# Cross attentions with 16 heads of 16: turning the exponents, or taking the scores a second time with keys on partitions

## The chip, the cores and the metric

The kernel runs on one core of a Trainium2 chip. The metric is the device time in microseconds (us) of one launch. Times of groups of instructions come from one profiled execution; a kernel's time is the median of its timed runs. The engines are TensorE (PE, its weight loads PEld), VectorE (DVE), ScalarE (ACT), GpSimd (POOL), and SyncE (SP), which starts DMAs.

## What is computed

The reference is a decoder of four layers on x of shape (8, 112, 256), each with a self attention, a cross attention and a feed-forward part, all in float32 but for a quantised last part. The change concerns the cross attentions of layers 1 and 3. Both attend from the 112 tokens of each batch to the 375 rows of a context of width 128, with 16 heads of 16:

```
B, LQ, D_MODEL = q.shape
...
qh = (q @ Wq + bq).reshape(B, LQ, HEADS, D_K).transpose(0, 2, 1, 3)
kh = (k @ Wk + bk).reshape(B, LKV, HEADS, D_K).transpose(0, 2, 1, 3)
vh = (v @ Wv + bv).reshape(B, LKV, HEADS, D_K).transpose(0, 2, 1, 3)
```

Then softmax(qh kh^T / 4) vh for each head, the heads joined, times Wo (plus bo), and added to x. Here q is the layer-normalised x, and k and v are both the context. Layer 3 has the same form without biases.

## The kernel before, in words

A class holds x on chip and runs the twelve sublayers in turn. `cross` (line 1098) serves three of them: layers 1 and 3 with heads of 16 (`dense`), and a part of layer 2 with heads of 32 that the change leaves as it is.

Work goes in 32 steps (b, c): b is one of 8 batches, c one of four chunks of four heads. A chunk's queries lie on 128 partitions, four strips of 32 rows. In the dense case two heads share the 32 rows of a key strip, so a batch has two key tiles of 128 rows instead of four; a query strip holds one head's 16 rows and zeros for the other's (`_halves`, line 79), and the order of heads that this needs (`_SLOTS`, line 71) is also applied to the value and output weights.

Before the loop come the keys and values of batch 0, `ln_T` (line 465: normalise half of the tokens, transpose them on TensorE, copy them), four query products for the first half of the tokens, and `ln_T` for the second half. This part is ordered by the framework's own scheduler. In the loop (lines 1250 to 1283) the order on TensorE, VectorE and ScalarE is the written one. One step does:

- `turn` (1183): for each of the chunk's four heads three transposes of the exponents (line 1187) into one of two PSUM banks "tr", then one copy to SBUF, on VectorE (1195) for even heads and on ScalarE (1193) for odd ones;
- `key` (1129) for the next batch in steps 0 and 2, `summed` (1215) in step 1, `divide` (1227) in step 3 for the batch before;
- `score` (1162) for the next step: four matmuls of 32 rows, queries stationary and keys moving, so that tokens lie on partitions and the 375 keys along the row; one PSUM bank each;
- `exponent` (1169): for each head the negated row maximum on VectorE (1174) and exp(score - maximum) on ScalarE (1178);
- `value` (1139) for the next batch in steps 0 to 2; two `query` products for the second half in step 3 of batches 0 and 1; `result` (1238) for the batch before in step 3: the output product and `finish`, here `add_to_x` (489);
- `attend` (1198): twelve matmuls, three chunks of 125 keys for each head, values (32 columns a head, column 16 holding ones, so that sums of exponents come along) stationary, exponents moving. After step 3 the outcome goes to SBUF on ScalarE (1213).

`summed` gathers the sums of exponents by four small matmuls, takes reciprocals (1222) and spreads them on POOL (1224); `divide` transposes them (1230) and multiplies (1236). Key, value, query, sums and result share a single PSUM bank "mm". All plain matmuls pass through the helper `mm`, and so carry its line, L410 in the profile.

Of the kernel before, what the change touches and what calls it, by code (L numbers as in the profile page):

```python
# [66 lines left out]

_SLOTS = [8 * (n // 2) + 2 * j + n % 2 for n in range(4) for j in range(4)]


def _slots(w):

    return w.reshape(-1, 16, 16)[:, _SLOTS].reshape(w.shape)


def _halves(w):

    out = np.zeros((w.shape[0], 4, 4, 2, 16), w.dtype)
    a = w.reshape(-1, 16, 16)[:, _SLOTS].reshape(-1, 4, 4, 16)
    for n in range(4):
        out[:, n, :, n % 2] = a[:, n]
    return out.reshape(-1, 512)
# [29 lines left out]
def _weights(inp):  # L115
    def g(layer):
# [49 lines left out]
            ("l1x_wq", _fm(_halves(xa("Wq")))),  # L166
            ("l1x_wk", xa("Wk")),
            ("l1x_wv", _slots(xa("Wv"))),
            ("l1x_bv", _row(_slots(xa("bv")[None])[0])),
        ],  # L170
        [
            ("l1x_wo", _fm(_spread(_slots(xa("Wo").T)).T)),
# [7 lines left out]
    for j in range(2):  # L180
# [4 lines left out]
        ("l1x_bq", _col(_halves(xa("bq")[None])[0])),  # L185
        ("l1x_bk", _col(xa("bk"))),
# [42 lines left out]
    v2 = [(f"l2f_{n}_s", _col(f(f"{n}_s"))) for n in ("w1", "w2", "h1", "h2")]  # L229
    for pf in ("a1", "a2"):  # L230
        for n in ("lnx_g", "lnx_b", "lny_g", "lny_b", "ln3_g", "ln3_b", "li2_b"):
# [12 lines left out]
            ("l3x_wq", _fm(_halves(xa("Wq").T))),  # L244
            ("l3x_wk", wkv[:, :D]),
            ("l3x_wv", _slots(wkv[:, D:])),
            ("l2f_w3_s", _row(inp["L2_ffn_w3_s"])),
        ],
        [("l3x_wo", _fm(_spread(_slots(xa("Wo"))).T))],
# [106 lines left out]
class _Kernel:  # L356
# [741 lines left out]
    def cross(self, name, cT, qsrc, wq, wk, wv, wo, hd, scale, finish, ctx, bq=None, bk=None, bv=None):  # L1098


# [18 lines left out]

        values = [self.t(acts, [P, NCH, 16, 32], f"xv{i}") for i in range(2)]  # L1120
        dense = hd == 16
        nk = 2 if dense else 4
        if dense:
            for v in values:
                nc.gpsimd.memset(v, 0.0)
                nc.gpsimd.memset(v[:CH, :, :, hd : hd + 1], 1.0)
        keys = {}

        def key(b, c):
            if c == 0:  # L1130
                keys[b] = self.t(work, [P, nk, CTX], "xkT")
            pm = self.t(ps1, [P, 512], "mm")[:, :CTX]
            self.mm(pm, [(wk[:, c * P : (c + 1) * P], cT[:, b * CTX : (b + 1) * CTX])])
            if bk is None:
                nc.scalar.copy(keys[b][:, c, :], pm)
            else:
                nc.scalar.activation(keys[b][:, c, :], pm, AF.Identity, bias=self.v(bk, c))

        def value(b, i):
            pm = self.t(ps1, [P, 512], "mm")[:CH, : 16 * hd]  # L1140
# [1094 lines left out]
```

## Time and profile before

| | us |
|---|---|
| three timed runs | 2417.11, 2418.55, 2422.47 (median 2418.55) |
| profiled execution, its own time | 2413.31 |
| its span in the trace | 2411.5 |
| layer 1's cross attention, first scores to first output product of the tail | 828.7 to 1003.1 |
| layer 3's cross attention, first scores to the tail's output product | 2121.2 to 2295.6 |
| one inner batch of either | 19.48 |

A row of the timeline gives the start and length in us, the engine, the line, the operation, the tile written and those read, their shapes (stationary, then moving), and the count; in brackets idle time before it and who ended it. A row of busy times gives a stretch, its length, then PE, PEld, DVE, ACT and POOL with counts, the granted TensorE clock, the DMA share and GB/s. "L1187" is a line of the kernel.

### The profile page before, as it was taken

What the parts mean: (1) busy time and instruction counts of PE and PEld (TensorE: products, weight loads), DVE (VectorE), ACT (ScalarE), POOL (GpSimd) and SP (SyncE); (2) the same over time, 40 slices, a digit from 0 to 9 for tenths busy, and PEclk for the clock granted to TensorE, in tenths of its full rate; (3) what the DMA queues carried; (4) which work ended last, traced back from release to release, by engine and by line L of the source; (5) the groups of instructions that cost most, each with busy time, mean ns of one, the idle gap of its engine ahead of it and who ended that gap; (6) DMA issues with size and microseconds to landing.
All of it is one profiled execution on the core that took longest, in us unless ns stands there. A gap on an engine that the chain in (4) does not pass through costs nothing.

```text
span 2411.5 us, 43235 instructions
## 1 busy us (share of the span) xinstructions
PE 2138.1 (89%) x17032; PEld 1268.5 (53%) x17032; DVE 1430.9 (59%) x3994; ACT 773.9 (32%) x2157; POOL 217.1 (9%) x415
## 2 busy tenths in 40 slices
PE   6999999989898899899898859899999999899944
PEld 3444444445556566646555536466655556556622
DVE  4655566565545567553888557767750133667787
ACT  2333334453211256430111211366321110246522
POOL 0111111000011100000222331100000000200000
PEclk9999999899999999999999989999999999899966
DMA  4000000000100000101001001000111100000000
GB/s 186 2 2 2 2 20 35 30 18 18 53 1 15 19 2 2 36 9 35 35 18 35 19 27 53 18 1 2 71 35 53 51 0 1 1 1 2 2 0 16
DMA packets 10730, 55.94 MB, mean 23 GB/s; under 512 B 1833, under 2 KB 3625, under 8 KB 5792
## 3 DMA queue, kind: packets, MB, share of 16 engines
q1 hardware_dynamic: 8304, 44.57, 5.2%
q0 software_dynamic: 2080, 7.07, 0.9%
q8 instruction: 135, 2.21, 0.4%
q10 hardware_dynamic: 144, 1.54, 0.2%
q14 instruction: 67, 0.55, 0.1%
HBM read 52.23 MB, written 0.92 MB: 22 GB/s over the span
## 4 chain that ended last, share of the span: by engine, by line
PE 67%; DVE 21%; issue 5%; ACT 4%; DMA 2%; POOL 1%; DVEq 0%; ACTq 0%; POOLq 0%
PE mm L410 31%; PE gu L410 6%; PE g L649 6%; PE tr L1187 6%; PE sc L410 4%; PE av L1203 3%; PE tr L410 2%; DVE rot L1496 1%; ACT sg L660 1%; PE av L786 1%; PE av L410 1%; ACT th L671 1%; DVE hT L675 1%; PE g L627 1%; PE s L410 1%
## 5 line engine op out<-in xcount | busy, mean ns | idle before, releaser
L649 PE MATMUL g<-w,hT 128*32 128x256 f32 x3552 | 237.3, 384 | 26.0 <-DVE hT L675 25.8
L1174 DVE TENSOR_REDUCE xnm<-sc 112x1 f32<-112x375 f32 x384 | 184.6, 541 | 28.5 <-PE sc L410 28.0
L1187 PEld LDWEIGHTS tr<-cst,xe 112*125 112x125 f32 x1152 | 151.5, 188 | 94.7 <-issue 37.9
L1187 PE MATMUL tr<-cst,xe 112*125 112x112 f32 x1152 | 192.9, 289 | 7.2 <-DVE xeT L1195 4.3
L410 PE MATMUL mm<-xnT,w 128*128 128x448 f32 x432 | 182.3, 559 | 18.8 <-DVE qT L1499 5.3
L410 PE MATMUL mm<-hT,w 128*128 128x448 f32 x512 | 193.0, 539 | 0.0
L649 PEld LDWEIGHTS g<-w,hT 128*32 128x32 f32 x3552 | 95.4, 109 | 168.1 <-DVE hT L675 124.9
L410 PEld LDWEIGHTS mm<-hT,w 128*128 128x128 f32 x512 | 97.1, 190 | 94.4 <-issue 94.4
L627 PE MATMUL g<-xw,cst 128*32 128x256 f32 x1792 | 138.0, 379 | 0.0
L1195 DVE COPY xeT<-tr 125x336 f32<-125x336 f32 x192 | 97.3, 507 | 67.6 <-PE tr L1187 60.7
L1193 ACT COPY xeT<-tr 125x336 f32<-125x336 f32 x192 | 85.4, 445 | 159.9 <-PE tr L1187 159.9
L410 PEld LDWEIGHTS mm<-xnT,w 128*128 128x128 f32 x432 | 77.8, 192 | 104.0 <-issue 54.0
L1178 ACT ACTIVATE xe<-sc,xnm 112x375 f32<-112x375 f32 x256 | 126.4, 582 | 11.2 <-DVE xnm L1174 11.2
L410 PE MATMUL mm<-w,hT 128*112 128x256 f32 x576 | 129.0, 383 | 0.0
L410 PE MATMUL gu<-xnT,w 128*128 128x448 f32 x320 | 126.1, 549 | 1.6 <-DVE hT L1341 1.2
L410 PE MATMUL mm<-w,oT 128*112 128x256 f32 x416 | 105.6, 404 | 22.2 <-DVE oT L1676 13.7
L410 PEld LDWEIGHTS mm<-w,hT 128*112 128x112 f32 x576 | 102.0, 179 | 25.3 <-issue 3.5
L660 ACT ACTIVATE sg<-g 128x192 f32<-128x192 f32 x224 | 74.1, 331 | 104.8 <-PE g L649 92.7
L671 ACT ACTIVATE th<-cell 128x64 f32<-128x64 f32 x224 | 57.4, 256 | 147.4 <-DVE cell L669 147.1
L410 PEld LDWEIGHTS mm<-w,oT 128*112 128x112 f32 x416 | 74.1, 186 | 52.1 <-DVE oT L1676 15.0
L2089 DVE COPY wq<-tr 128x256 bf16<-128x256 bf16 (+1 forms) x12 | 4.6, 420 | 162.9 <-PE tr L2088 162.9
L673 DVE TENSOR_TENSOR h<-sg,th 128x64 f32<-128x64 f32 x224 | 50.6, 226 | 85.5 <-ACT th L671 85.5
(402 smaller groups left out, 3631.4 us busy)
## 6 DMA issues: line engine op xcount, KB each, us to landing
w<-in_w SPq DMA_DIRECT2D x33, 1024.0 KB, 4.9
raw<-in_wq POOLq DMA_DIRECT2D x3, 1024.0 KB, 5.1
w<-in_w SPq DMA_DIRECT2D x3, 896.0 KB, 6.8
wi<-in_wint POOLq DMA_DIRECT2D x3, 768.0 KB, 6.2
w<-in_w SPq DMA_DIRECT2D x2, 768.0 KB, 4.1
ctxT<-in_ctxT ACTq DMA_DIRECT2D x1, 1500.0 KB, 8.3
cx<-in_ctx POOLq DMA_DIRECT2D x1, 1500.0 KB, 20.8
w<-in_w SPq DMA_DIRECT2D x2, 512.0 KB, 3.6
```

What stands on the lines that cost most here:

```text
L410: self.nc.tensor.matmul(out, lhsT, rhs, start=i == 0, stop=i == len(pairs) - 1)
L627: nc.tensor.matmul(g[32 * j : 32 * j + 32, :], pick[:, t % 16, :], xw[:, l, t // 16, 256 * j : 256 * j + 256], start=True, stop=t == 0, sk ...
L649: nc.tensor.matmul(g[32 * j : 32 * j + 32, :], hT[l][:, c, :], whh[l][:, c, 256 * j : 256 * j + 256], start=False, stop=c == 1, skip_group ...
L660: nc.scalar.activation(sg[:, :192], g[:, :192], AF.Sigmoid)
L671: nc.scalar.activation(th, cell[l], AF.Tanh)
L673: nc.vector.tensor_tensor(h, og, th, ALU.mult)
L1174: nc.vector.tensor_reduce(nm, sc, AX.X, ALU.max, negate=True)
L1178: nc.scalar.activation(e, sc, AF.Exp, bias=nm)
L1187: nc.tensor.transpose(tp[:CH, i * S : (i + 1) * S], e[:, i * CH : (i + 1) * CH], self.ident[:S, :S])
L1193: nc.scalar.copy(eT, src)
L1195: nc.vector.tensor_copy(eT, src)
L1203: nc.tensor.matmul(avs[b][32 * j : 32 * j + 32, c * S : (c + 1) * S], values[b % 2][:CH, i, 4 * c + j, :], eTs[b, c, j][:, i, :], start=i ...
```

## The change

The dense case leaves `cross` and gets a function of its own, `cross_twice`. Keys get one strip of 32 rows a head, as queries have: 16 rows of data, row 16 set to one by the bias (`_SHIFT`), and zeros. The head orders `_SLOTS` and `_halves` go.

- `score` as before, but the four heads write one PSUM tile of four banks, and `maxima` takes two heads' negated maxima by one VectorE instruction, into column 16 of a head's 32.
- `shifted` transposes these, so that they come to lie in row 16 of each strip, and adds them to the queries.
- `exponent` takes the scores again, keys stationary (125 at a time) and shifted queries moving: the row of ones brings in the negated maximum. Keys now lie on partitions, as `attend` needs them, and ScalarE takes the exponential of two heads at a time straight from PSUM. `turn`, with its transposes and copies, is gone.
- `key` runs in every step, with a bias in both layers; `attend` lags by a step, `result` by a batch and a step; the queries of the second half are spread over four steps.
- PSUM: one "sc" tile of four banks, one "sT" of two, "mm" and "av" one each. Token transposes before the loop use "mm" too.

The core of the diff: the weights, then the new function.

```diff
-            ("l1x_wq", _fm(_halves(xa("Wq")))),
-            ("l1x_wk", xa("Wk")),
-            ("l1x_wv", _slots(xa("Wv"))),
+            ("l1x_wq", _fm(_spread(xa("Wq")))),
+            ("l1x_wk", _spread(xa("Wk"))),
+            ("l1x_wv", xa("Wv")),
...
-        ("l1x_bk", _col(xa("bk"))),
+        ("l1x_bk", _col(_spread(xa("bk")[None])[0] + _SHIFT)),
...
+    v2 = [("l3x_bk", _col(_SHIFT))]
...
+    def cross_twice(self, name, wq, wk, wv, wo, bk, finish, ctx, bq=None, bv=None):
+        nc, tc, cT = self.nc, self.tc, self.ctxT
+        acts = ctx.enter_context(tc.tile_pool(name=f"{name}_q", bufs=1))
+        work = ctx.enter_context(tc.tile_pool(name=f"{name}_w", bufs=2))
+        ps1 = ctx.enter_context(tc.tile_pool(name=f"ps1_{name}", bufs=1, space=PSUM))
+        values = [self.t(acts, [P, NCH, 16, 32], f"xv{i}") for i in range(2)]
+        nms = [self.t(acts, [P, 4, 32], f"xn{i}") for i in range(2)]
+        for t in values + nms:
+            nc.gpsimd.memset(t, 0.0)
+        for v in values:
+            nc.gpsimd.memset(v[:CH, :, :, 16:17], 1.0)
+        qT = self.t(acts, [P, 4, T], "qT")
+        keys, scs, qas, eTs, avs, oTs, sums = {}, {}, {}, {}, {}, {}, {}
+        def mm():
+            return self.t(ps1, [P, 512], "mm")
+        def key(b, c):
+            if c == 0:
+                keys[b] = self.t(work, [P, 4, CTX], "xkT")
+            pm = mm()[:, :CTX]
+            self.mm(pm, [(wk[:, c * P : (c + 1) * P], cT[:, b * CTX : (b + 1) * CTX])])
+            nc.scalar.activation(keys[b][:, c, :], pm, AF.Identity, bias=self.v(bk, c))
+        def value(b, i):
+            pm = mm()[:CH, :D]
+            at = b * CTX + i * CH
+            self.mm(pm, [(cT[:, at : at + CH], wv)])
+            src, dst = pm.rearrange("p (h d) -> p h d", h=16), values[b % 2][:CH, i, :, :16]
+            if bv is None:
+                nc.vector.tensor_copy(dst, src)
+            else:
+                nc.vector.tensor_tensor(dst, src, bv[:CH].rearrange("p (h d) -> p h d", h=16), ALU.add)
+        def query(half, c):
+            cols = slice(half * HT, (half + 1) * HT)
+            pm = mm()[:, :HT]
+            self.mm(pm, [(wq[:, k, c * P : (c + 1) * P], self.xnT[:, k, cols]) for k in range(2)])
+            if bq is None:
+                nc.vector.tensor_scalar(qT[:, c, cols], pm, 0.25, None, ALU.mult)
+            else:
+                nc.vector.tensor_scalar(qT[:, c, cols], pm, self.v(bq, c), 0.25, ALU.add, ALU.mult)
+        def rows(j):
+            return slice(32 * j, 32 * j + 32)
+        def score(b, c):
+            scs[b, c] = self.t(ps1, [P, 4, 512], "sc")
+            for j in range(4):
+                self.mm(scs[b, c][:S, j, :CTX], [(qT[rows(j), c, b * S : (b + 1) * S], keys[b][rows(j), c, :])])
+        def maxima(b, c):
+            for h in (0, 2):
+                nc.vector.tensor_reduce(
+                    nms[c % 2][:S, h : h + 2, 16], scs[b, c][:S, h : h + 2, :CTX], AX.X, ALU.max, negate=True
+                )
+        def shifted(b, c):
+            tp = scs.pop((b, c))[:, 0, 384 : 384 + S]
+            nc.tensor.transpose(tp, nms[c % 2][:S].rearrange("p j d -> p (j d)"), self.ident[:S, :S])
+            qas[b, c] = self.t(work, [P, S], "xqa")
+            nc.vector.tensor_tensor(qas[b, c], tp, qT[:, c, b * S : (b + 1) * S], ALU.add)
+        def exponent(b, c, h):
+            sT = self.t(ps1, [P, 2, 512], "sT")
+            for i in range(NCH):
+                for j in range(2):
+                    r = rows(h + j)
+                    self.mm(sT[:CH, j, i * S : (i + 1) * S], [(keys[b][r, c, i * CH : (i + 1) * CH], qas[b, c][r, :])])
+            eTs[b, c, h] = self.t(work, [P, 2, NCH * S], f"xeT{h}")[:CH]
+            nc.scalar.activation(eTs[b, c, h], sT[:CH, :, : NCH * S], AF.Exp)
+        def attend(b, c):
+            if c == 0:
+                avs[b] = self.t(ps1, [P, 512], "av")
+            for i in range(NCH):
+                for j in range(4):
+                    nc.tensor.matmul(
+                        avs[b][rows(j), c * S : (c + 1) * S],
+                        values[b % 2][:CH, i, 4 * c + j, :],
+                        eTs[b, c, j & 2][:, j & 1, i * S : (i + 1) * S],
+                        start=i == 0,
+                        stop=i == NCH - 1,
+                        skip_group_check=True,
+                    )
+            if c == 3:
+                oTs[b] = self.t(work, [P, 4, S], "xoT")
+                nc.scalar.copy(oTs[b], avs.pop(b)[:, : 4 * S].rearrange("p (c s) -> p c s", c=4))
+        def summed(b, sm):
+            for i in range(4):
+                self.mm(sm[:, 4 * i : 4 * i + 4], [(oTs[b][:, i, :], self.c("sums"))])
+            ri = self.t(self.small, [P, 16], "xri")[:S]
+            nc.vector.reciprocal(ri, sm)
+            sums[b] = self.t(work, [P, 16, 32], "xrw")[:S]
+            nc.gpsimd.tensor_copy(sums[b], ri[:, :, None].to_broadcast([S, 16, 32]))
+        def divide(b):
+            tp = mm()
+            for c in range(4):
+                nc.tensor.transpose(
+                    tp[:, c * S : (c + 1) * S],
+                    sums[b][:, 4 * c : 4 * c + 4, :].rearrange("p h d -> p (h d)"),
+                    self.ident[:S, :S],
+                )
+            oT = oTs[b]
+            nc.vector.tensor_tensor(oT, tp[:, : 4 * S].rearrange("p (c s) -> p c s", c=4), oT, ALU.mult)
+        def result(b):
+            oT = oTs.pop(b)
+            finish(b, self.project(ps1, b, [oT[:, c, :] for c in range(4)], wo))
+        for c in range(4):
+            key(0, c)
+        for i in range(NCH):
+            value(0, i)
+        self.ln_T(ps1, 0, "mm")
+        for c in range(4):
+            query(0, c)
+        self.ln_T(ps1, 1, "mm")
+        steps = [(b, c) for b in range(NB) for c in range(4)]
+        ends = {(0, 3): 0, (1, 0): 1, (1, 2): 2, (2, 2): 3}
+        with tc.manual_schedule(engines={ET.PE, ET.DVE, ET.Activation}):
+            score(0, 0)
+            maxima(0, 0)
+            for n, (b, c) in enumerate(steps):
+                more = n + 1 < len(steps)
+                shifted(b, c)
+                if b + 1 < NB:
+                    key(b + 1, c)
+                if more:
+                    score(*steps[n + 1])
+                    maxima(*steps[n + 1])
+                exponent(b, c, 0)
+                if 0 < c < 3 and b + 1 < NB:
+                    value(b + 1, c)
+                if c == 3 and b > 0:
+                    divide(b - 1)
+                if n > 0:
+                    attend(*steps[n - 1])
+                if c == 0 and b + 1 < NB:
+                    value(b + 1, c)
+                exponent(b, c, 2)
+                if c == 0 and b > 1:
+                    result(b - 2)
+                if c == 1 and b > 0:
+                    summed(b - 1, scs[steps[n + 1]][:S, 1, 384:400])
+                if (b, c) in ends:
+                    query(1, ends[b, c])
+            attend(*steps[-1])
+            result(NB - 2)
+            summed(NB - 1, mm()[:S, :16])
             divide(NB - 1)
             result(NB - 1)
```

## The prediction

> **What bounds the kernel now.** I read the page's first part, then its groups by form, then the timeline of TensorE over one batch of the first of the two cross attentions that change, and last the busy times of the same stretch.
>
> ```profile
> PE 2138.1 (89%) x17032; PEld 1268.5 (53%) x17032; DVE 1430.9 (59%) x3994; ACT 773.9 (32%) x2157; POOL 217.1 (9%) x415
> ```
>
> TensorE (PE) leads, but this is an average over twelve stages. The stage is read from the batch that follows, with start, duration, and what was issued. I work with differences of starts, because durations of pipelined matmuls overlap. A matmul in float32 is two entries, its two passes; a transpose is one.
>
> ```profile
> 899.21 0.91 PE L1187 MATMUL tr<-cst,xe 112*125 112x112 f32 x6
> 899.95 0.81 PE L410 MATMUL mm<-ctxT,w 128*128 128x375 f32 x2
> 900.60 0.48 PE L1187 MATMUL tr<-cst,xe 112*125 112x112 f32 x3
> 901.01 0.90 PE L410 MATMUL sc<-xkT,qT 32*112 32x375 f32 x8
> 901.84 0.58 PE L1187 MATMUL tr<-cst,xe 112*125 112x112 f32 x3
> 902.25 0.61 PE L410 MATMUL mm<-w,ctxT 128*125 128x256 f32 x2
> 902.79 0.97 PE L1203 MATMUL av<-xeT,xv 125*32 125x112 f32 x24
> ...
> 912.81 0.91 PE L1187 MATMUL tr<-cst,xe 112*125 112x112 f32 x6
> 914.08 0.57 PE L1230 MATMUL tr<-cst,xrw 112*128 112x112 f32 x4 [0.36 <-DVE xeT L1195]
> 914.49 0.49 PE L1187 MATMUL tr<-cst,xe 112*125 112x112 f32 x3
> 914.91 0.90 PE L410 MATMUL sc<-xkT,qT 32*112 32x375 f32 x8
> 915.74 0.58 PE L1187 MATMUL tr<-cst,xe 112*125 112x112 f32 x3
> 916.16 1.89 PE L410 MATMUL mm<-w,xoT 128*112 128x256 f32 x8
> 917.98 0.78 PE L1203 MATMUL av<-xeT,xv 125*32 125x112 f32 x24
> ```
> ```profile
> 899.21:918.69 19.48, 19.12 (x210) 13.34 (x206) 14.52 (x33) 12.33 (x28) 0.62 (x1) 1.00 0.01 2
> ```
>
> Seven groups follow one another with no marked wait: a step is the sum of TensorE's own issue times. Four steps take 4.48, 4.64, 4.48 and 5.88 us, in all 19.48 us a batch, and the same 19.48 or 19.49 returns for every undisturbed inner batch of both attentions. In the last row the columns are PE, PEld, DVE, ACT and POOL, then the granted clock: 19.12 of 19.48 us for PE at full clock, 14.52 for VectorE, 12.33 for ScalarE. So only TensorE's work, and waits that reach it, count. Relief of VectorE and ScalarE is worth nothing by itself.
>
> **What a piece costs TensorE, from these starts.** Key product 0.65, value product 0.54, first scores 0.83, six transposes 0.74, three 0.42, result 1.82. The weighted sum (av) takes 0.90 where it follows soon after the last copy of exponents, and 0.71 (917.98 to the next transposes at 918.69) where that copy is long done. Inside a run of transposes the pitch is 0.109 with 125 columns loaded.
>
> **Taken away, a step:** twelve transposes, 0.74 + 0.42 + 0.42 = 1.58; 0.19 of waiting in av, since av now lags by a step; at the fourth step the 0.53 before 914.08, where the division waits for a copy (1.27 from 912.81 against 0.74). On VectorE two copies of 0.507, on ScalarE two of 0.445, and the four separate exponentials.
>
> **Added: the second scores.** Twelve matmuls a step, as two groups of six that use two 32-row strips each. No row has this shape. The nearest is the score of the first self attention, two 64-row strips alternating:
>
> ```profile
> 495.14 1.04 PE L746 MATMUL s<-kT,qT 64*112 64x112 f32 x16
> 496.11 0.98 PE L778 MATMUL tr<-cst,e 112*112 112x112 f32 x8
> ```
>
> Eight passes a strip in 0.97. The sixteen-head self attention has four strips, also eight passes a strip (x32), and takes 0.98 (750.64 to 751.62): time goes by passes per strip, not by matmuls. That is the point on which the sum hangs: with two strips at work instead of four, twelve matmuls cost about double. A pass of 112 columns is 0.097 (the key's two of 375 take 0.65); eight make 0.78, and 0.19 is left for start and end. Here 125 columns are loaded for each pass, so I take the 0.109 of the transposes, which load as many: 6 x 0.109 + 0.19 = 0.84. The first of the two groups follows the first scores, which use the same strips, and saves the end and start between them (0.2): 0.64. Together 1.48 a step.
>
> Two rules of the Trainium skill weigh here. "TensorE: Matmul & The Clock Gate", Part 3 (The mechanism), says a weight load overlaps running matmuls only when its row group differs. Taken strictly, a strip would load (by that page's columns/1.2 rule an estimate of 104 ns) and then stream (97 ns), 0.2 a pass, and a group would cost 1.4 instead of 0.84: about +1 us a step, +64 us for both attentions. The rows speak against that: eight passes a strip in 0.97 leave room for 0.12 each. I take the row. "TensorEngine Tiling (Array Packing)", Key Properties, says that changing the tiling mode drains the engine. The row prices it: of the 0.19 I put half, 0.09, to the end of one mode and half to the first weight load of the next. Without it a step would be some 0.3 shorter; I count it.
>
> **Added: the rest.** A key product in every step (heads are spread to 32 rows, so four key tiles a batch, not two). A transpose of the negated maxima, 112x128. Transpose and key together 0.2 + 0.63 + 0.09 drain = 0.92. Value now stands after a change of mode: 0.62. Division 0.5 instead of 0.41. A step with value is then 0.92 + 0.83 + 0.64 + 0.62 + 0.71 + 0.84 = 4.56. By steps: first 4.56 + result 1.72 + 0.50 = 6.78, second 4.56 + sums 0.72 = 5.28, third 4.56, fourth 3.94 + 0.50 = 4.44. The 0.50 is a new wait: result now ends the step and the next key product wants the single "mm" bank, which VectorE must first empty by add_to_x (0.42 and two hand-overs of about 0.1, less the transpose of 0.2 in front). Behind that key stand the scores. Sum 21.06 against 19.48: **+1.58 a batch**.
>
> Waits that are added and should be hidden. Scores of step n+1 wait for VectorE's addition (128x112, about 0.28 by the 0.625 of 448 columns and 0.425 of 256): transpose to addition to score is about 0.75, under the 0.92 of transpose and key. The next transpose waits for the maxima: two reductions of 750 elements, each about 0.94 (541 ns for 375, 618 for 448), done 0.93 + 1.87 = 2.8 after the scores start, while TensorE works 3.5 to 3.6 there. Second group waits for ScalarE's exponential of the first (672 columns, about 0.72 by 546 for 448 and the slope of its copies): done 2.35 after the scores start, TensorE arrives at 2.7 to 2.8. If any of these covers fails, its excess lands in every step. VectorE falls to about 11 us a batch, ScalarE to about 9; both have room. The memsets on POOL and four more columns of constants cost nothing: two tiles of 128x128 against 1.38 for 128x1536 that already runs under the previous stage. The key's copy on ScalarE comes twice as often, in the second attention now with a bias (574 ns for 473); it is done under the first scores. The key weights double to 128x512 in a block that is fetched ahead: no wait on a DMA shows among this stretch's waits.
>
> **By batch.** Batch 0 (833.68 to 855.14 before): three steps 4.1, 4.6, 4.6, last 3.9 and one query with its wait for the bank 2.3 = 19.5 against 21.46: -2.0. Batch 1: 4.6 + 2.3, 5.3, 4.6 + 2.3, 4.4 (no result yet) = 23.5 against 24.58: -1.1. Batch 2: 21.1 + 2.3 against 19.49: +3.9. Batches 3 to 6: 4 x 1.58 = +6.3. Batch 7 has no key and no value, but nothing to cover the addition (0.55 a step) and one result more, which in turn hides the last copy: +1.6. Sum +8.7.
>
> **Before the loop.** Keys, values, queries and now also the token transposes pass through one bank, each with its hand-over:
>
> ```profile
> 820.24 0.70 PE L410 MATMUL mm<-w,ctxT 128*125 128x256 f32 x2 [0.67 <-ACT xkT L1137]
> 821.51 0.70 PE L410 MATMUL mm<-w,ctxT 128*125 128x256 f32 x2 [0.57 <-DVE xv L1147]
> ```
>
> A key holds the bank 1.56 (818.68 to 820.24), a value 1.27, a token transpose about 1.25. Two keys more and four transposes that had banks of their own: 3.1 + 5.0 = 8.1. The bounds are 0 (all of it hidden while the earlier stage ends) and 8.1. Before, the first key holds its bank from 813.52 to 818.68, 3.6 longer than 1.56, behind the earlier stage's last result; half of that may be used, so I take 6.
>
> Sum 8.7 + 6 = 14.7 an attention, 29.4 for two. The profiled execution took 2413.31 (span 2411.5, 1.8 around it) and would become 2443; it lies 5 under the median of 2418.55, and on that it is **2448**.
>
> **Rivals.** The forecast, TensorE still the bound with slightly more work: 0.60.
> *Faster, 0.15:* the array overlaps the two strips of a group with its neighbours, so that twelve second scores cost as four strips do, 24/32 of 0.98 = 0.74 a step. That is 0.74 x 64 = 47 us less than I count: 2401. For it: strips are independent in the rows above. Against: 64-row strips, just as independent, did not gain. It turns faster than before once a step's second scores fall below 1.48 - 29.4/64 = 1.02.
> *A chain takes the place of the engine, 0.14:* scores and second scores have one buffer each, so maxima, transpose, addition, scores run in series. For it: every link has a hand-over. Against: 0.7 us of slack a step. It decides from 0.7 on; with hand-overs 1.4 longer than I count, 0.7 a step reaches TensorE: +45, 2493.
> *No difference, 0.11:* start hidden (6), 0.098 instead of 0.109 a pass (0.53 a batch, 4.2), no bank wait after six results (3): +1.5 an attention, 2422.
>
> **Range.** 2408 to 2480 leaves out most of the fast rival and the far end of the chain. A measurement here tells about 0.2%, 4.8 us, from no change. Faster 0.15, within 0.11, slower 0.74.
>
> **What would show it.** Right: inner batches near 21 us at an unbroken TensorE, a group of twelve second-score instructions holding it 0.6 and 0.8, key waiting about 0.5 after result, the loop starting some 6 us later. Wrong: batches under 19.5 with second scores under 1.0 a step (the fast rival), or marked waits of the nm transpose on the maxima, or of the scores on the addition, in every step (the chain).

## The result, and the profile after

The changed kernel takes 2499.98 us (median of four runs, 2498.49 to 2502.66) against 2417.83 for the kernel before (four runs, 2416.83 to 2422.47). The ratio is 1.0335, with a 95% interval of 1.0318 to 1.0353. The forecast was 2448, with a range that ended at 2480: the sign was right, the size was not. The loss is 82 us, not 29. Below, an execution over 1.5% longer than the shortest of its kernel is listed but not compared; there are three, all of kernels with second scores in two strips.

The profiled execution took 2502.66, 89.35 more than that of before. First the page's busy row, then its row of the granted clock in 40 slices:

```profile
PE 2208.5 (88%) x17928; PEld 1307.2 (52%) x17928; DVE 1375.5 (55%) x3802; ACT 715.5 (29%) x1933; POOL 216.6 (9%) x419
PEclk9999999999899899799998989999999998799866
```

TensorE grew by 70 us, of which part is the same work done at a lower clock; VectorE and ScalarE fell by 55 and 58, as the change means them to. In the clock row the 14th and 17th slices (8 and 7) lie in layer 1's attention, where before had 9s; the 35th and 38th (7 and 8) lie in layer 3's, where before had 8 and 9.

An undisturbed inner batch of the first attention answers to the batch shown of before. Timeline of TensorE, from one output product on:

```profile
946.92 0.26 PE L1306 MATMUL sc<-cst,xn 112*128 112x112 f32 x1
947.60 0.90 PE L392 MATMUL mm<-ctxT,w 128*128 128x375 f32 x2 [0.42 <-DVE x L475]
948.43 0.90 PE L392 MATMUL sc<-xkT,qT 32*112 32x375 f32 x8
949.15 0.80 PE L392 MATMUL sT<-xqa,xkT 32*125 32x112 f32 x12
949.89 0.70 PE L392 MATMUL mm<-w,ctxT 128*125 128x256 f32 x2
950.51 0.78 PE L1325 MATMUL av<-xeT,xv 125*32 125x112 f32 x24
951.23 0.91 PE L392 MATMUL sT<-xqa,xkT 32*125 32x112 f32 x12
952.07 0.95 PE L392 MATMUL sc<-cst,xoT 128*112 128x4 f32 x8
953.37 0.32 PE L1306 MATMUL sc<-cst,xn 112*128 112x112 f32 x1 [0.35 <-DVE xri L1342]
```

By differences of starts, the two groups of second scores (sT) take 0.74 and 0.84, the first scores 0.72, the value 0.62, the weighted sum 0.72. The key's wait after the output product is there (0.42). From one output product to the next there are 21.75 us, forecast were 21.06. The last line holds what the forecast lacked: the sums of exponents (952.07) are written into the tile of the first scores, and the transpose of the maxima, in the same tile, waits until VectorE has read them. Sums to transpose takes 1.30 instead of the 0.72 in my sum: +0.58 a batch.

The rest is not in such a batch. I cut each attention into three stretches: A from the last copy of the self attention before it to the loop's first transpose, B from there to the first transpose of batch 7, C from there to the last output product. The clock in the trace is 1.00 or 0.50; the lower rows give the time at 0.50, the half clock.

| us, layer 1 / layer 3 | A | B | C |
|---|---|---|---|
| before | 19.6 / 17.8 | 145.7 / 144.3 | 23.7 / 23.3 |
| after | 32.9 / 30.2 | 161.1 / 169.8 | 32.1 / 32.2 |
| added | 13.3 / 12.4 | 15.4 / 25.5 | 8.4 / 8.9 |
| forecast | 6 | 7.1 | 1.6 |
| at half clock, before | 2.8 / 2.2 | 3.4 / 0 | 1.9 / 0 |
| at half clock, after | 20.0 / 19.1 | 3.4 / 23.9 | 15.0 / 15.1 |

The added 83.9 are nearly all of the 89.35. The half clock in these stretches grew from 10.3 us to 96.5. Work takes nearly twice as long at half clock (below, a query 3.35 instead of 1.77), so the 86 us more are worth 43 at most, an estimate: less where TensorE waited anyway. Forecast (29), the sums' waits (0.58 in 14 batches, 8) and this 43 make 80 of the 84. Here A, the start: keys, then queries, then the first transpose of maxima, token transposes of the second half, and the next batch's key.

```profile
820.26 0.90 PE L392 MATMUL mm<-ctxT,w 128*128 128x375 f32 x2 [0.80 <-ACT xkT L1268]
...
832.23 3.35 PE L392 MATMUL mm<-xnT,w 128*128 128x448 f32 x4 [0.62 <-ACT xnT L387]
836.36 3.36 PE L392 MATMUL mm<-xnT,w 128*128 128x448 f32 x4 [0.78 <-DVE qT L1287]
...
847.56 0.29 PE L1306 MATMUL sc<-cst,xn 112*128 112x112 f32 x1 [0.35 <-DVE xn L1299]
...
849.38 0.60 PE L459 MATMUL mm<-cst,xn 112*128 112x112 f32 x4 [0.72 <-DVE xnT L385]
850.60 0.90 PE L392 MATMUL mm<-ctxT,w 128*128 128x375 f32 x2 [0.62 <-ACT xnT L387]
```

Each product waits 0.5 to 0.8 for the bank, as counted. But a query takes 3.35, where before had 1.77 (in its queries from 824.43 to 833.68, the first of which stands here):

```profile
824.43 1.77 PE L410 MATMUL mm<-xnT,w 128*128 128x448 f32 x4
```

Rows of busy times over A and C, with the clock in the sixth column after the length:

```profile
827.80:844.80 17.00, 14.37 (x28) 5.64 (x28) 2.66 (x5) 0.53 (x1) 0.00 (x0) 0.50 0.00 0
...
1001.80:1022.30 20.50, 18.39 (x269) 13.54 (x270) 10.26 (x19) 6.89 (x11) 0.61 (x1) 1.00 0.14 53
1022.30:1036.00 13.70, 12.82 (x119) 9.60 (x109) 1.91 (x4) 3.35 (x5) 0.00 (x0) 0.50 0.01 1
1036.00:1039.40 3.40, 1.63 (x12) 1.15 (x12) 1.15 (x4) 0.00 (x0) 0.61 (x1) 1.00 0.00 0
1039.40:1045.00 5.60, 4.34 (x12) 2.54 (x10) 1.06 (x3) 0.00 (x0) 0.00 (x0) 0.50 0.00 0
```

The clock is 0.50 or 1.00, for stretches that are multiples of 3.4 us. In batch 7 (timeline) there is no key to cover the addition, and soon everything runs at half speed:

```profile
1009.32 0.90 PE L392 MATMUL sc<-xkT,qT 32*112 32x375 f32 x8 [0.37 <-DVE xqa L1308]
...
1015.26 0.90 PE L392 MATMUL sc<-xkT,qT 32*112 32x375 f32 x8 [0.60 <-DVE xqa L1308]
...
1019.88 0.32 PE L1306 MATMUL sc<-cst,xn 112*128 112x112 f32 x1 [0.42 <-DVE xri L1342]
...
1033.06 3.40 PE L392 MATMUL mm<-w,xoT 128*112 128x256 f32 x8
```

An output product, 1.98 at full clock (945.11), takes 3.40. In B there are single stretches of 3.4 us at half clock, and in layer 3 a longer one at the loop's start (2182.9 to 2193.1).

### The profile page after: what moved, and what is told of

It reads as the page before. It is cut to its first block, busy times and chain, and to the rows that moved or that the text cites. A ratio compares the mean times of both kernels' runs of the same rounds, so it can differ in the third digit from the quotient of the medians.

```text
span 2500.9 us, 44067 instructions
## 1 busy us (share of the span) xinstructions
PE 2208.5 (88%) x17928; PEld 1307.2 (52%) x17928; DVE 1375.5 (55%) x3802; ACT 715.5 (29%) x1933; POOL 216.6 (9%) x419
## 4 chain that ended last, share of the span: by engine, by line
PE 67%; DVE 21%; issue 5%; ACT 4%; DMA 1%; POOL 1%; DVEq 0%; ACTq 0%; POOLq 0%
PE mm L392 32%; PE gu L392 6%; PE g L631 6%; PE sc L392 5%; PE sT L392 4%; PE tr L1147 2%; PE av L1325 2%; PE tr L392 1%; DVE rot L1616 1%; ACT sg L642 1%; PE av L768 1%; PE av L392 1%; ACT th L653 1%; DVE hT L657 1%; PE s L392 1%
## 5 line engine op out<-in xcount | busy, mean ns | idle before, releaser
L392 PE MATMUL mm<-xnT,w 128*128 128x448 f32 x432 | 188.8, 575 | 17.3 <-DVE qT L1619 4.9
L1299 DVE TENSOR_REDUCE xn<-sc 112x2 f32<-112x750 f32 x128 | 114.3, 936 | 87.2 <-PE sc L392 87.2
L1318 ACT ACTIVATE xeT<-sT 125x672 f32<-125x672 f32 x128 | 93.6, 731 | 165.8 <-PE sT L392 164.0
L392 PE MATMUL mm<-w,oT 128*112 128x256 f32 x416 | 106.0, 405 | 23.6 <-DVE oT L1796 13.7
L392 PEld LDWEIGHTS sT<-xqa,xkT 32*125 32x125 f32 x1536 | 106.5, 196 | 35.3 <-issue 13.7
L392 PE MATMUL sT<-xqa,xkT 32*125 32x112 f32 x1536 | 117.4, 287 | 2.3 <-ACT xeT L1318 2.3
L392 PE MATMUL sc<-xkT,qT 32*112 32x375 f32 x768 | 95.5, 548 | 2.7 <-DVE xqa L1308 2.7
L475 DVE TENSOR_TENSOR x<-mm,x 112x256 f32<-112x256 f32 x64 | 27.1, 423 | 124.7 <-PE mm L392 124.7
## 6 DMA issues: line engine op xcount, KB each, us to landing
cx<-in_ctx POOLq DMA_DIRECT2D x1, 1500.0 KB, 20.5
```

What stands on the lines that cost most here:

```text
L392: self.nc.tensor.matmul(out, lhsT, rhs, start=i == 0, stop=i == len(pairs) - 1)
L475: nc.vector.tensor_tensor(self.x[:S, b, :], ps, self.x[:S, b, :], ALU.add)
L1299: nc.vector.tensor_reduce(nms[c % 2][:S, h : h + 2, 16], scs[b, c][:S, h : h + 2, :CTX], AX.X, ALU.max, negate=True)
L1318: nc.scalar.activation(eTs[b, c, h], sT[:CH, :, : NCH * S], AF.Exp)
```

## Experiments

The theory after this: TensorE's work is what I counted, and the 53 us beyond it are waits (one bank at the start, the sums' tile, the bare batch 7) together with the half clock that they bring. The rivals are that the waits alone cost it, or that the clock answers to something else than waits. The first is already unlikely: the output product at 1033.06 has no marked wait and takes 3.40 instead of 1.98.

**Three banks at the start.** In A, keys, values, token transposes and queries take three tiles in turn:

```diff
         def mm():
-            return self.t(ps1, [P, 512], "mm")
+            if not start[0]:
+                return self.t(ps1, [P, 512], "mm")
+            turn[0] += 1
+            if turn[0] % 3 == 0:
+                return self.t(ps1, [P, 2, 512], "sT")[:, 0, :]
+            return self.t(ps1, [P, 512], ("mm", "av")[turn[0] % 3 - 1])
...
```

> The part before the loop of the changed kernel, with its keys, values, token transposes and queries spread over three banks in turn instead of one. Theory A (most of the loss at the start is the single bank's hand-overs and the half clock that the idle TensorE is given after them): the first transpose of negated maxima comes 10 to 15 us earlier in layer 1's cross attention and 8 to 12 in layer 3's, the granted clock between keys and loop stays above 0.8, and the total falls by 20 to 30 from 2500, to 2470 to 2480. Rival B (the start waits for normalisation and copies on VectorE and ScalarE, not for the bank): under 3 an attention, total 2494 to 2500.

Measured: 2487.01 (2486.33 to 2502.58; ratio to before 1.0312, 1.0276 to 1.0347). The timeline of TensorE shows products with no mark of a wait:

```profile
824.12 1.46 PE L392 MATMUL sT<-ctxT,w 128*128 128x375 f32 x2
...
831.17 1.67 PE L392 MATMUL av<-xnT,w 128*128 128x448 f32 x4
```

A falls from 32.9 to 22.4 and from 30.2 to 18.1, what theory A says (the clock, though, stood at 0.50 for 9.6 us of it in layer 1). The total fell by 13 only, not by 20 to 30. The profiled execution was the longest of the four, 2502.58, so its B shows where such a gain can go: 176.4 and 177.8 instead of 161.1 and 169.8. The half clock now lies in the loop (busy times):

```profile
905.20:918.90 13.70, 13.11 (x81) 7.64 (x75) 3.43 (x6) 2.35 (x4) 0.00 (x0) 0.50 0.00 0
919.00:956.30 37.30, 35.76 (x450) 25.01 (x447) 18.84 (x36) 14.63 (x22) 0.92 (x2) 1.00 0.01 2
956.40:966.70 10.30, 10.30 (x71) 6.16 (x71) 2.63 (x5) 2.61 (x4) 0.21 (x1) 0.50 0.00 0
```

The last row holds no idle time at all, at clock 0.50. That spoke against waits as the cause, and led to the runs on the array's use below.

**Fillers at the start, and their control.** The order of A on TensorE is written out, with or without extra products:

```diff
+        fl = self.t(ps1, [P, 4, 512], "sc")
+        def filler(n):
+            for _ in range(n):
+                nc.tensor.matmul(fl[:, 3, :128], wk[:, :P], cT[:, :128], start=True, stop=True)
+        with tc.manual_schedule(engines={ET.PE}):
             for c in range(4):
                 key(0, c)
+                filler(3)
...
```

> The changed kernel with its single bank at the start, the start's order on TensorE written out, and two or three extra matmuls of 128x128 after each key, value, token transpose and query, into the unused PSUM tile and read by nobody: hand-overs stay, only TensorE's idle time is filled. Theory A (the clock falls because TensorE idles): against the same kernel without the fillers the granted clock at the start rises from about 0.5 to over 0.8 and the loop begins 4 to 8 us earlier, total 8 to 15 lower. Rival B (hand-overs alone are the cost): no gain, or a loss of up to 5 an attention since the fillers stand in the way, total 0 to 10 higher.

> The control for the fillers: the same written order at the start, no filler. Both theories: within 5 of the changed kernel's 2500, clock about 0.5 to 0.6 in the queries' stretch. If it differs by more, the order in which the second half's tokens stand ahead of the first step's keys is a cost of its own.

Measured: 2501.33 with fillers, 2502.97 without. Busy times, the first row from the control, the next two from the kernel with fillers:

```profile
818.00:843.80 25.80, 19.20 (x32) 7.58 (x34) 7.36 (x23) 2.83 (x5) 2.96 (x4) 0.50 0.11 41
```
```profile
816.50:846.20 29.70, 26.64 (x145) 18.52 (x149) 11.77 (x28) 3.63 (x7) 2.97 (x4) 1.00 0.11 36
846.20:863.30 17.10, 17.10 (x116) 11.09 (x110) 5.66 (x9) 4.38 (x7) 0.00 (x0) 0.50 0.00 1
```

The fillers do hold the clock at 1.00, and a query with its hand-over falls from 4.1 to 2.55. A is 2.9 shorter than the control's in layer 1 and no shorter in layer 3. But the two differ in more than the fillers: these write the tile of the first scores, so that here all scores and the second half's token transposes come after the queries, and the first transpose waits 2.07 for the maxima, where the control waits 0.32. Up to the loop's first key product, which both reach with the same work done, the kernel with fillers is 5.8 and 2.8 shorter. The clock then falls at the loop's start, in a row without idle time. The total shows nothing: theory A was right on the clock, about right on the loop's start in layer 1, and wrong on the 8 to 15.

**Sums in another bank.**

```diff
-                    summed(b - 1, scs[steps[n + 1]][:S, 1, 384:400])
+                    summed(b - 1, avs[b][:S, 448:464])
```

> The changed kernel with the sums of exponents gathered in the bank of the weighted sums instead of in the tile of the first scores. Theory (the transpose of negated maxima waits for the reciprocal of the sums because both are the same tile): its wait in step 1 of a batch falls from 1.30 to about 0.72, inner batches from 21.75 to 21.15, seven batches an attention, total 8 lower (2492). Rival: the wait moves to the division or to the weighted sum that shares the new bank, total unchanged within 3.

Measured: 2478.69 (2473.14 to 2499.54; ratio 1.0278, 1.023 to 1.0326), 21 lower. Timeline of step 1:

```profile
954.73 0.95 PE L392 MATMUL av<-cst,xoT 128*112 128x4 f32 x8
955.53 0.29 PE L1306 MATMUL sc<-cst,xn 112*128 112x112 f32 x1
955.66 0.81 PE L392 MATMUL mm<-ctxT,w 128*128 128x375 f32 x2
```

The wait is gone, an inner batch takes 21.23: 0.52 shorter, forecast 0.6. That is 7 of the 21. The rest goes with the half clock: this profile has none of it in B, where after has one window in layer 1 and five stretches in layer 3; B is 155.7 and 155.4. That is the loop at full clock: 10.0 and 11.1 over before, where the forecast has 7.1 and where the second half's token transposes, which before had ahead of the loop, put nearly 3 (847.56 to 850.60 above).

**A key product in batch 7.**

```diff
-            self.mm(pm, [(wk[:, c * P : (c + 1) * P], cT[:, b * CTX : (b + 1) * CTX])])
+            at = min(b, NB - 1) * CTX
+            self.mm(pm, [(wk[:, c * P : (c + 1) * P], cT[:, at : at + CTX])])
...
-                if b + 1 < NB:
-                    key(b + 1, c)
+                key(b + 1, c)
```

> The changed kernel with a key product more in each step of the last batch (the last batch's keys once more, into a tile that nobody reads), so that the addition is covered there as in other batches. Theory A (the tail is long because TensorE's waits in batch 7 bring the half clock, 3.41 us at a time): the extra work costs 4 x (0.74 - 0.37) = 1.5 an attention, but the last batch and tail run at full clock, 36.4 becomes 30 to 32, total 5 to 10 lower, 2490 to 2495. Rival B (the waits cost their own length only): total 0 to 4 higher, 2500 to 2504.

Measured: 2488.63 (2484.53 to 2505.26; ratio 1.0295, 1.0248 to 1.0342). More work, less time. C falls from 32.1 and 32.2 to 27.8 in both. Busy times of batch 7, to be set beside the rows of after from 1001.8 on:

```profile
1012.20:1022.00 9.80, 8.78 (x92) 6.04 (x92) 3.44 (x8) 3.34 (x5) 0.61 (x1) 1.00 0.01 2
1022.00:1035.50 13.50, 10.63 (x147) 7.71 (x143) 4.08 (x9) 4.03 (x6) 0.61 (x1) 1.00 0.23 79
```

Idle time on TensorE is no smaller here (2.9 of 13.5, against 0.9 of 13.7), but the clock is 1.00.

**The three edits together.** The diffs for the start's banks, for the sums and for batch 7 in one kernel.

> The changed kernel with the three earlier edits together: three banks in the part before the loop, sums in the bank of the weighted sums, a further key product in the last batch. Theory (what is left over the kernel before is TensorE's own work, some 1.2 to 1.6 a batch and the two keys more at the start): inner batches 21.2 without longer ones, start 11 shorter an attention, total 2445 to 2460. Rival (the half clock falls wherever TensorE waits, and moves with the waits): single batches of 24 to 27 stay, total 2465 to 2480.

Measured: 2457.28 (2450.31 to 2477.41; ratio 1.0156, 1.0105 to 1.0208): 43 of the 82 are gone. A is 20.0 and 18.1, near before's; B 154.3 and 160.1, inner batches 21.24; C 27.3. The kernel before took 2420.34 on the same chip, so 37 are left, near the forecast of 29. That nearness is partly luck. The 29 held 12 for the start, which this kernel no longer pays (0.4 and 0.3); B and C cost 32 more than before where 17 were forecast, with 16 us more at half clock (8 at most) and the extra keys (3 by the expectation) in them.

**Two strips or four.** Is the price of the second scores the strips? Two kernels leave out the first scores, maxima, transpose and addition; they differ in the second scores:

```diff
-            sT = self.t(ps1, [P, 2, 512], "sT")
+            sT = self.t(ps1, [P, 4, 512], "sT")
             for i in range(NCH):
-                for j in range(2):
+                for j in range(4):
...
```

> The changed kernel without the first scores, maxima, transpose and addition: the exponentials are taken of the scores as they are, so the subtraction of the row maximum is left out. The two groups of six matmuls of two strips stay, and key, value and the rest; sums in the bank of the weighted sums. Theory (TensorE's work is the bound): a step loses the first scores 0.72 and the transpose 0.15 to 0.2, gains 0.1 to 0.2 where the first group no longer follows scores in the same strips, so a batch is 2.8 to 3.2 shorter than 21.2, near 18.2, and the total 2380 to 2410. Rival (maxima, addition and banks in series set the step): a batch falls below 17, total under 2370.

> As the kernel without first scores and without the subtraction of the maximum, but its twelve second-score matmuls are one group that goes round all four strips in four banks, with both exponentials after it. Theory (time goes by passes a strip, so two strips cost double): a group of twelve takes 0.75 to 0.85 instead of 0.73 + 0.84, a batch is 2.5 to 3.2 shorter than with two strips, total 40 to 50 lower. Rival (the fast rival of the prediction: strips overlap with neighbours anyway): less than 0.3 a batch, total within 10. A third way: with one buffer of four banks the exponentials now end on TensorE's path, a marked wait of the group on ScalarE, and the gain is eaten.

Measured: two strips 2485.71 (2457.09 to 2508.42), four strips 2379.27 (2377.05 to 2392.65; ratio 0.9832, 0.9798 to 0.9866). Inner batches take 18.83 and 16.00. The timelines, first with two strips (from a later run of that kernel), then with four:

```profile
953.85 0.91 PE L392 MATMUL sT<-qT,xkT 32*125 32x112 f32 x12
954.69 0.70 PE L392 MATMUL mm<-w,ctxT 128*125 128x256 f32 x2
```
```profile
907.65 0.92 PE L392 MATMUL sT<-qT,xkT 32*125 32x112 f32 x24
908.50 0.70 PE L392 MATMUL mm<-w,ctxT 128*125 128x256 f32 x2
```

Six matmuls (x12) in two strips hold TensorE 0.84, twelve (x24) in four strips 0.85: time goes by passes per strip, as the forecast priced it, and the rival that strips overlap with neighbours is dead. The 2.83 a batch make 45 us. Both kernels missed their totals, though: the medians lie 106 apart (105 without the execution of 2508.42) instead of 40 to 50, with the two strips slower than the 2380 to 2410 expected. Where much of the other 60 went shows here (busy times of the two-strip kernel, layer 3, then layer 1 of a later run of it):

```profile
2165.00:2240.00 75.00, 72.84 (x465) 46.22 (x464) 5.73 (x12) 18.79 (x28) 0.61 (x1) 0.50 0.00 1
```
```profile
845.80:886.80 41.00, 39.47 (x242) 23.99 (x242) 2.85 (x6) 10.91 (x17) 0.00 (x0) 0.50 0.00 1
```

TensorE is 97% busy for 75 us, at half clock throughout. So being busy does not bring the clock back; perhaps how much of the array works does. These two loops began at half clock and kept it for 77 and 39 us. In the later run layer 3's loop began at full clock, and kept that until batch 7, 2303.3:

```profile
2165.50:2240.00 74.50, 70.02 (x815) 45.97 (x814) 11.69 (x27) 31.91 (x48) 1.84 (x3) 1.00 0.01 2
```

**Bursts of full rows.** The two-strip kernel with four bursts:

```diff
...
                 exponent(b, c, 2)
+                if c == 1 and b < 2:
+                    for _ in range(4):
+                        nc.tensor.matmul(fl[:, 3, :], wk[:, :P], cT[:, :512], start=True, stop=True)
```

> As the kernel without first scores and with second scores in two strips (the maximum is not subtracted there), plus a burst of four products of 128x512 that use the whole array, written to an unused bank and read by nobody, in step 1 of batches 0 and 1: four bursts in all. In the kernel without them TensorE was 97% busy for 75 us at granted clock 0.50. Theory A (the clock answers to how much of the array works in a 3.41 us window, and two strips of four keep it down; a window of full rows brings it back): the half clock ends with the first burst, the bursts cost 4 x 3.4 to 6.8 = 14 to 27, the cold stretches of about 40 and 75 shrink to under 20 each, total 2435 to 2465 against 2486. Rival B (the clock answers to waits of TensorE, which the bursts do not take away): cold stretches stay, total 14 to 27 higher, 2500 to 2515.

Measured: 2478.72 (2473.77 to 2482.19), between what the two theories say. The stretches of 41 and 78 became 0 and 17 in the profiled execution, but a new one came (2267.4 to 2287.9). The 0 is not owed to the bursts: this loop began at full clock, 6.5 us ahead of the first burst (859.36), after 31 us at half clock before it. Only the 17 in layer 3, which ends in its first burst, can be.

```profile
846.00:887.00 41.00, 36.11 (x329) 21.13 (x328) 5.48 (x10) 13.21 (x20) 0.00 (x0) 1.00 0.01 1
```

The timeline ahead of the new stretch has no mark of a wait:

```profile
2263.99 0.91 PE L392 MATMUL sT<-qT,xkT 32*125 32x112 f32 x12
2264.83 0.95 PE L392 MATMUL av<-cst,xoT 128*112 128x4 f32 x8
2265.64 0.88 PE L392 MATMUL mm<-ctxT,w 128*128 128x375 f32 x2
2266.44 0.91 PE L392 MATMUL sT<-qT,xkT 32*125 32x112 f32 x12
2267.28 1.15 PE L392 MATMUL mm<-w,ctxT 128*125 128x256 f32 x2
```

What stands there are half-filled second scores and the sums, whose matmuls have four columns moving, and TensorE is busy in the whole window of 3.41 us before the fall. The 17 and the new stretch speak for the array's use, the total for neither.

**Idle strips filled.** This run is meant to change neither waits nor, by passes per strip, TensorE's time; beside each second score another is issued in a strip that would idle:

```diff
+                for j in range(2):
+                    r = rows(2 - h + j)
+                    self.mm(fl[:CH, 2 - h + j, :S], [(keys[b][r, c, i * CH : (i + 1) * CH], qT[r, c, b * S : (b + 1) * S])])
                 for j in range(2):
                     r = rows(h + j)
...
```

> As the kernel without first scores and with second scores in two strips (the maximum is not subtracted there), but beside each of these matmuls another is issued in a strip that would idle, with the same shape, into a bank that nobody reads: twice the second-score instructions, all four strips at work. Theory A (time goes by passes per strip, and the half clock comes from an array half empty): an undisturbed batch stays at 18.8, within 0.4, the cold stretches of 41 and 78 shrink to under 20, and the kernel with more work is faster than its control by 20 to 70. Rival B (the half clock comes from waits): batch and cold stretches as in the control, total within 10 of it. Rival C (strips do not overlap fully): a batch of 20 to 22 us, total 20 to 50 above the control.

> The kernel without first scores and with second scores in two strips once more, beside the one with idle strips filled. Both theories: 2457 to 2508 as before, median near 2486, with cold stretches of some 40 to 80 us in the first batches.

Measured: filled 2436.45 (2433.17 to 2438.07; ratio 1.0075, 1.006 to 1.009), control on the same chip 2459.11 (2448.39 to 2517.95; ratio 1.0152, 1.0125 to 1.0179). Without its executions of 2509 and 2518 the control lies between 2448 and 2467, median 2451: the kernel with more work is 15 us faster, clear of noise, though less than the 20 to 70 of theory A. An inner batch takes 18.95, against 18.83, with twice as many second scores. Layer 1's loop decides nothing here, since it began at full clock, as with the bursts. Layer 3's began at half clock, and lost it after 8.3 us:

```profile
2153.30:2161.60 8.30, 8.30 (x79) 5.53 (x78) 0.42 (x1) 3.34 (x5) 0.00 (x0) 0.50 0.01 2
2161.60:2200.00 38.40, 36.25 (x608) 24.09 (x608) 5.31 (x11) 15.92 (x24) 0.61 (x1) 1.00 0.01 2
```

The loops of two strips that began so stayed there for 39, 77 and 39 us, and the one of four strips for 8.5. In batch 7 all the profiled two-strip loops fell to half clock (for 13 us and more, bursts or not), the filled ones only at their last product. So filling the idle strips, at nearly equal time a batch, shortens the half clock. It doubles the count of matmuls too, and no run parts that from the array's use. In the changed kernel itself this could not be tried, since its eight banks are taken.

**Parts of the change alone, on the kernel before.** First the lag of the weighted sum by a step:

```diff
                 turn(b, c, 1)
+                if dense and n > 0:
+                    attend(*steps[n - 1])
...
-                attend(b, c)
+                if not dense:
+                    attend(b, c)
...
```

> The kernel before, with one idea of the change alone: in the two cross attentions with heads of 16 the weighted sum lags by a step, so that it no longer waits for the last copy of exponents. By the prediction's prices a batch saves three times 0.19 of waiting in av and up to 0.53 at the division: 1.1 at most, 16 for both attentions, 2402 to 2410. Rival (the wait of av is not the copy but the change of array mode, and the division's wait stays): nothing, 2416 to 2422.

Measured: 2443.76 (2437.7 to 2452.91; ratio 1.0095, 1.0069 to 1.0121). Slower, and neither expectation came true. Timeline:

```profile
909.68 1.04 PE L1187 MATMUL tr<-cst,xe 112*125 112x112 f32 x6 [0.61 <-ACT xe L1178]
910.65 0.78 PE L1203 MATMUL av<-xeT,xv 125*32 125x112 f32 x24
```

The sum takes 0.71 as priced, but at its old place it had covered ScalarE's exponentials. Without it the transposes wait 0.61 in three steps of four; a batch takes 21.33. With the sum lagging but left at its place:

```diff
...
-                attend(b, c)
+                if not dense:
+                    attend(b, c)
+                elif c > 0:
+                    attend(*steps[n - 1])
...
```

> The kernel before with the weighted sum lagging by a step, but left at its place at the end of a step (in a batch's first step ahead of the value product), so that it still covers the exponentials that the next step's transposes wait for. In the run with the sum moved ahead, it took 0.71 instead of 0.90, and the transposes waited 0.61 for ScalarE in three steps of four. Theory: 0.19 a step is saved and no wait is added, a batch takes 18.7 to 18.9 instead of 19.48, total 8 to 12 lower, 2408 to 2413. Rival: the exponentials end later than the shortened sum, the 0.19 comes back as a wait of the transposes, total within 3 of the kernel before.

Measured: 2443.41 (2441.85 to 2447.61; ratio 1.0096, 1.0078 to 1.0115); undisturbed batches take 20.29. Neither expectation came true here either: theory had 18.7 to 18.9 a batch, the rival a total within 3 of before. A later outcome now reaches its reader late:

```profile
914.31 0.85 PE L410 MATMUL mm<-cst,xoT 128*112 128x4 f32 x7 [0.77 <-ACT xoT L1213]
```

The third part, token transposes through the single bank:

```diff
-        qsrc(ps, 0)
+        one = (ps1, 0, "mm") if dense else (ps, 0)
+        qsrc(*one)
...
-        qsrc(ps, 1)
+        qsrc(one[0], 1, *one[2:])
```

> The kernel before with another part of the change alone: the token transposes before the loop of the two dense cross attentions go through the single bank of keys, values and queries. By the prediction four hand-overs of 1.25 in each attention, of which part is hidden: 0 to 5 an attention, total 2418 to 2428. Theory with the half clock (TensorE waits more, and a window at half clock follows): 6 to 12 an attention, total 2430 to 2444.

Measured: 2433.11 (2425.16 to 2446.62; ratio 1.0054, 1.0039 to 1.0069). That is what the theory with the half clock expected (2430 to 2444). A grows by 4.8 and 4.7, though only the first half's two transposes lie in it; the second half's now stand behind the loop's first transpose. Half clock in A grows from 2.8 and 2.2 us to 9.8 and 9.0, worth 3.5 of the 4.8 at most. The first query after the transposes shows it:

```profile
828.18 3.21 PE L410 MATMUL mm<-xnT,w 128*128 128x448 f32 x4 [0.62 <-ACT xnT L405]
```

So one part of the change, on the kernel before, brings hand-overs and the half clock together.

## Why the prediction was wrong, step by step

- **TensorE is the bound, and a step is the sum of its groups: right.** Second scores 0.74 + 0.84 against 0.64 + 0.84, first scores 0.72 against 0.83, value and weighted sum within 0.01, transpose and key 0.89 against 0.92, the output product with its wait and the next transpose 2.49 against 2.42 (the product alone 1.81; the sum took 1.72, where its own row of before reads 1.82). The kernel with sums elsewhere has 21.23 a batch, forecast 21.06.
- **Passes per strip: right**, shown by 0.84 and 0.85, and by 18.95 against 18.83; a group did not take the 1.4 of the strict reading. The 0.19 a group for its start and end was not measured apart from the passes.
- **Maxima, addition and exponentials hidden: right while there is a key.** The chain rival did not come about.
- **"Value ... sums 0.72": a wait was missed.** Sums and maxima share a tile; +0.58 in seven batches, 8 us for both attentions.
- **"Before the loop": the waits were about right, the clock was left out.** From the last copy to the loop's first key, when the transposes of both halves are done, there are 36.0 and 33.2 us instead of 20.5 and 18.7: 15.5 and 14.5 more, where I took 6. Of these, 20.0 and 19.6 us stand at half clock (before 2.8 and 2.2), which is worth 8.6 and 8.7 at most. The 6.9 and 5.8 that are left are near the 6.
- **"Batch 7 ... +1.6": the same.** The bare additions were counted at 0.55 and waited 0.37 to 0.60, so the waits were right. The half clock that set in was not foreseen: C costs 8.4 and 8.9, with 13 and 15 us more at half clock, worth 6.6 and 7.6 at most. With a key in place it is 4.1 and 4.5, extra work included.
- **The step that failed is the assumption behind all of these: "19.12 of 19.48 us for PE at full clock" was carried over to a kernel with more waits and emptier groups.** I priced these in time and put what they do to the clock at nothing, without a reason. The traces show 86 us more at half clock in its place, worth 43 at most of the 53 that were missed; most of the other 10 are the sums' waits.

That the half clock costs time is shown by equal work at both clocks (a query 3.35 and 1.77); that it costs up to 43 of the 82 is a sum over the traces, not a run. What brings it on in particular batches of the changed kernel is not shown run by run. In layer 3, B is 8.7 longer than in layer 1 and has 20.5 us more at half clock, worth 10.2 at most: that can hold it, and is argued. Of the 89, 5.5 us lie outside the three stretches, 4.1 of them between the two attentions, where 11 us more stand at half clock; that can hold them too. The one kernel that beats both, second scores in four strips at 2379.27, leaves out the subtraction of the maximum; none that keeps it beats the kernel before.

## What to carry to other kernels

Price a TensorE group twice: its time (passes per strip), and what it does to the clock, because a loop of groups in two strips of four kept the half clock for 39 to 77 us where fuller groups lost it after 8. When a resource is narrowed to one buffer before a loop, count the hand-overs (the waits until a reader has emptied the bank), and then ask what the clock will be: here it cost about as much again. A matmul that only seems to wait may be covering another engine: the lag of the weighted sum saved 0.19 and uncovered 0.61.

## What the runs showed of the hardware

The granted clock moved in steps of 3.41 us between 1.00 and 0.50, and did not answer to TensorE being busy alone. It stood at 0.50 for 75 us with TensorE 97% busy, and fell after a window in which TensorE was busy throughout (2263.97 to 2267.38 of the kernel with bursts). The Trainium skill ("TensorE: Matmul & The Clock Gate", Part 1) has it fall after an idle window and return after a busy one. These runs differ, and the measurement decides.

The two-strip loop kept whichever clock it began with: 0.50 for 39, 77 and 39 us, or, in two loops, 1.00 up to the last batch. The kernels with filled or with four strips left 0.50 after 8.3 and 8.5 us.

As a check on all 16 traces I worked out, for each window of 3.41 us, the share of the array at work: rows times columns used times columns streamed (at the key's pace, 750 in 0.65 us), of all that fits in. Of 10025 windows at full clock 475 were followed by a half one. One bound, a share under 0.33, leaves 124 of the 10025 on the wrong side; the share of rows alone leaves 136, TensorE's busy time 198, and expecting no fall at all 475. For the return to full clock the share does no better than busy time (224 and 228 wrong of 1368). This is a count by shapes, an estimate, with the bound fitted to the same windows, and no run set that share by itself.
